# Two graph layers in f32 on one core: the order of the opening steps is changed

## The chip, the cores and the metric

The kernel runs on one core of a Trainium2 chip. The metric is the device time of one execution in microseconds (us); lower is better. The kernel before took a median of 2537.88 us in four runs (2536.48 to 2541.1).

## What is computed

For 64 graphs of 256 nodes with 512 features, two layers follow each other. Each normalises x, applies relu, runs an attention over the same adjacency, and adds the result to x.

```python
h = jnp.maximum(_layernorm(x, axis=-1), 0.0)
x = x + _L0_gnn_ref(h, adj, L0_gnn_W, L0_gnn_a)
h = jnp.maximum(_layernorm(x, axis=-1), 0.0)
x = x + _L1_gnn_ref(h, adj, Wq, bq, Wk, bk, Wv, bv, Wo, bo)
```

Layer 0 forms `h W`, a score for each edge from two columns (`a`), a leaky relu, a masked softmax, and the weighted sum; its output is that sum beside `h W`. Layer 1 is a masked attention with eight heads, with projections q, k, v and an output projection. All arithmetic is in f32.

## The kernel before

**Groups.** The 64 graphs ("batches") are worked in 32 groups of two (`GB`, `NG`). One group passes through these stages:

- `first_norm(g)` (L495 on): statistics of x on VectorE, `rstd` and `less` on GpSimd (`factors`), the normalised `xn` on ScalarE (`norm`), a transposition (`turn`), and the copy `hT0` on ScalarE (`put`). For group 0 the transposition is done by TensorE (tile `pt`). For later groups VectorE turns 32x32 blocks (`xt`, one buffer), a DMA writes them to DRAM (`passed`) and four DMAs bring them back (`moved`, `fetch`).
- `first_layer(g)`: four products `ph` (r0 to r3, two for each batch, with two extra columns for the edge scores), the edge scores `pn` and their exponentials `e`, and four weighted sums `po`, each followed on VectorE by a reciprocal, an add to x and the statistics of the second norm. Then the second norm in the same manner, which ends in `hT1` and in four `operand_sums` on GpSimd (tile `sums`).
- `project(g)`: q, k and v, each from seven products of half size (a Strassen scheme) in the order 1, 2, 6, 7, 5, 4, 3. Products 1, 6, 5 and 3 write one bank (`first`), 7 and 4 another. ScalarE copies a bank out (`take`; the copies that are kept are `kept_q` and so on) before the next product may rewrite it: product 6 waits for the copy of product 1, product 5 for that of 6, product 4 for that of 7. Product 6 is the first one that needs `sums`.
- `scores`, `weigh` and `outputs` (tiles `sc`, `total`, `pr`, `py`): the attention and its output projection.

**Checks on the weights.** `judge()` bounds the sizes of the weights, so that a softmax without a maximum can be used. It forms a gram matrix of the q and of the k weights (`gram_q`, `gram_k`, 32 matmuls each), squares each three times (`square_q`, `square_k`), adds up squares of weights on ScalarE, and ends in a small matmul and a few tiny operations on VectorE and GpSimd. Its verdict is read at the end of the kernel.

**What sets the order.** The order of TensorE's matmuls is the order of the code: each is tied to the one before (`in_order`, helper lines L137 and L140). The functions are generators, and the code at L808 to L890 says by hand which piece comes next. On the other engines most operations are tied behind the last recorded one by `not_sooner`; those that are not tied are placed by the scheduler, and can stand ahead of earlier ones in the code. Each engine works through its finished order one by one. In the opening (groups 0 and 1 in front of the main loop), `order` gives for each product i of `project(0)` what follows it: `n` a piece of `first_norm` (generator `norms`), `s` a piece of `first_layer(1)`; after it comes a piece of `judge()`. At i of 2, 8 and 15 VectorE forms sums of the k, v and o weights (`weight_sums`), and at i of 15 GpSimd adds the last bias to group 0's x (`residual`). In the main loop, `steps` says the same for each quarter of a group: `S` scores, `u` a product of the next group's projections, `o` a piece of the outputs, `s` and `n` as above for the groups two and three further on. All loads are issued on SP's queue, in the order of the code unless a wait lets another go ahead.

Of the kernel before, what the change touches and what calls it, by code (L numbers as in the profile page):

```python
# [10 lines left out]
AF = mybir.ActivationFunctionType  # L11
# [46 lines left out]
def bounded(  # L58
# [24 lines left out]
    vector, scalar, gpsimd, sync = (  # L83
        Remembers(e) for e in (nc.vector, nc.scalar, nc.gpsimd, nc.sync)
    )
# [12 lines left out]
    scale = 1.0 / DH**0.5  # L98
# [10 lines left out]
    def mm(name):  # L109
        return psum.tile([P, 512], F32, tag="turn", name=name, bufs=5)  # L110

    def held_bank(n, name):
        return psum.tile([P, 512], F32, tag=f"held{n}", name=name, bufs=1)

    def after(instruction, name):

        tc.add_manual_dep(
            instruction.ins, name,
            mybir.DependencyInfo(mybir.DependencyClass.NoSync, mybir.DependencyReason.DATA),
            reason="the engine's order",  # L120
        )

    def not_sooner(engine, operation, *args, **kwargs):

        last = engine.last
        after(getattr(engine, operation)(*args, **kwargs), last)
# [9 lines left out]
    def matmul(*args, **kwargs):  # L136
        in_order(nc.tensor.matmul(*args, **kwargs))  # L137
# [9 lines left out]
    def load(g, b):  # L147
        xs[g, b] = big.tile([P, NT, D], F32, tag="x", name=f"x{g}_{b}", bufs=8)
        if g == 2:
            not_sooner(sync, "dma_start", xs[g, b], xg[g, b])  # L150
        else:
            sync.dma_start(xs[g, b], xg[g, b])

    load(0, 0)


    ident = const.tile([P, P], F32, name="ident")
# [7 lines left out]

    w0_sb = const.tile([P, HP, F1 + 2], F32, name="w0_sb")
    nc.sync.dma_start(w0_sb[:, :, 2:], w0.rearrange("(c p) o -> p c o", p=P))
    load(0, 1)
    adj_i = att.tile([P, NT, N], I32, tag="kept", name="adj_i")
    nc.sync.dma_start(adj_i, adj.rearrange("(t p) k -> p t k", p=P))  # L170

# [49 lines left out]
    bcol = {}  # L221
# [30 lines left out]
    def weight_sums(name):  # L252
        w = w_sb[name]
        not_sooner(vector, "tensor_sub", w[:, :, T3, :], w[:, :, W22, :], w[:, :, W12, :])
        vector.tensor_sub(w[:, :, T1, :], w[:, :, W12, :], w[:, :, W11, :])
        vector.tensor_sub(w[:, :, T2, :], w[:, :, W22, :], w[:, :, T1, :])
        vector.tensor_sub(w[:, :, T4, :], w[:, :, W21, :], w[:, :, T2, :])
# [356 lines left out]
    def residual(g):  # L614

        for b in range(GB):
            for t in range(NT):
                xt = xs[g, b][:, t, :]
                not_sooner(gpsimd, "tensor_add", xt, xt, b_out)
# [4 lines left out]
    def place(shape, name):  # L624
        tag = places.pop(0)
        return big.tile(shape, F32, tag=tag, name=name, bufs=1), tag
# [4 lines left out]
    def project(g):  # L631
        ops = operands.pop(g)
        for name in ("q", "k", "v"):
            shape = [P, NT, D] if name == "v" else [P, HP, N]
            dst = {}
            for b in range(GB):
                dst[b], tag = place(shape, f"{name}_{g}_{b}")
                qkv[name, g, b] = dst[b], tag
            turn[0] = 1 - turn[0]

            def blocks(bank):
                return bank.rearrange("p (o n) -> p o n", o=2)

            def product(out, i, start):
                a, w = ops[i][0], w_sb[name][:, :, ops[i][1], :]
                for o in range(2):
                    cols = slice(o * P, (o + 1) * P)
                    for c in range(2):
                        of, by = (a[:, c, cols], w[:, c, :]) if name == "v" else (w[:, c, cols], a[:, c, :])
                        matmul(  # L650
                            out[:, o, :], of, by, start=start and o == c == 0, stop=o == c == 1,
                            skip_group_check=True,
                        )

            def part(b, half):
                if name == "v":
                    return dst[b][:, :, half * D // 2 : (half + 1) * D // 2]
                return dst[b][:, 2 * half : 2 * half + 2, :]

            def take(to, bank, half):  # L660
                if name == "v":
                    scalar.copy(to, bank)
                    return
                for o in range(2):
                    i = 2 * half + o
                    scalar.activation(
                        to[:, o, :], bank[:, o, :], AF.Identity,
                        bias=bcol[name][:, i : i + 1], scale=1.0,
                    )

            def kept(bank, half, i):
                s = att.tile([P, 2, N], F32, tag="kept", name=f"kept{i}_{name}_{g}")
                take(s, bank, half)
                return s

            first = blocks(held_bank(turn[0], f"p{name}1_{g}"))
            product(first, 1, True)
            p1 = kept(first, 0, 0)
            yield
            second = blocks(mm(f"p{name}2_{g}"))  # L680
            product(second, 2, True)
            vector.tensor_add(part(0, 0), second, p1)
            yield
            product(first, 6, False)
            p16 = kept(first, 0, 1)
            yield
            second = blocks(held_bank(1 - turn[0], f"p{name}7_{g}"))
            product(second, 7, True)
            p7 = kept(second, 1, 2)
            yield  # L690
            product(first, 5, False)
            vector.tensor_add(part(1, 1), first, p7)
            yield
            product(second, 4, False)
            vector.tensor_add(part(1, 0), second, p16)
            yield
            product(first, 3, False)
            take(part(0, 1), first, 1)
            yield

# [103 lines left out]
    def run(part):  # L804
        for _ in part:
            pass

    verdict = judge()  # L808
    norms = (piece for g in range(NG) for piece in first_norm(g))
    bias, edges = last_bias(), mask()  # L810
# [6 lines left out]
    for piece, _ in enumerate(first_layer(0)):  # L817
        if piece == 1:
            next(norms)
            next(norms)  # L820
            next(edges)
        elif piece == 2:
            next(norms)
        elif piece == 3:
            next(norms)
            late_loads()
        elif piece in (4, 7, 10):
            next(verdict)
            next(verdict)
            if piece == 10:  # L830
                next(norms)
                next(norms)
                weight_sums("q")
        elif piece == 11:
            next(products)
            next(products)
# [2 lines left out]
    next(norms)  # L839
    next(verdict)  # L840
    next(verdict)
    order = "n - - - nss s s - ss ss s sn n n - sn n n s".split()
    for i, parts in enumerate(order, 2):
        next(products)
        if i in (2, 8, 15):
            weight_sums("kvo"[i // 7])
        for part in parts:
            if part != "-":
                next(norms if part == "n" else pieces, None)
        next(verdict, None)  # L850
        if i in (6, 9, 11):
            next(bias)
        if i == 15:
            residual(0)
# [5 lines left out]
    for g in range(NG):  # L860
        products = project(g + 1) if g + 1 < NG else iter(())
        pieces = first_layer(g + 2) if g + 2 < NG else iter(())
        for step, parts in enumerate(steps):
            b, quad = divmod(step, NQ)
            if waiting is not None:
                weigh(*waiting)
                if waiting[2] == NQ - 1:
                    late = outputs(*waiting[:2])
            for part in parts:
                if part == "u":  # L870
                    next(products, None)
                elif part == "o":
                    next(late, None)
                elif part == "s":
                    next(pieces, None)
                elif part == "n":
                    next(norms, None)
                else:
                    waiting = (g, b, quad, *scores(g, b, quad))
            if step == 0 and g + 1 < NG:  # L880
                residual(g + 1)
            if step % 2 == 0 and g + 3 < NG:
                load(g + 3, b)
        run(products)
        run(pieces)
# [373 lines left out]
```

## Time and profile before

| what | value |
|---|---|
| median of four runs | 2537.88 us |
| the profiled execution's own time | 2537.21 us |
| its span in the profile | 2535.4 us |
| mean granted TensorE clock | 0.998 |
| matmuls | 16158 |
| DMA, mean over the span | 81 GB/s |
| first matmul of group 0's `pt` | 8.42 us |
| first scores `sc` | 97.81 us |
| first `ph` of group 2 | 125.11 us |
| last matmul begins its run at | 2528.74 us |

The profile is that of one execution. PE is TensorE, PEld its weight loads, DVE VectorE, ACT ScalarE, POOL GpSimd, and SP the engine that issues DMAs. A timeline row gives the start, the time until the last of a run of like operations ended, the engine, the line, the operation, the tile that it writes and those that it reads, the shape and the count; in brackets the idle time of the engine before it and what ended it. Nearly all operations show a helper's line (L35, L137, L140), so that the tile's name tells them apart. All times count from the start of the span.

### The profile page before, as it was taken

The numbers are of one execution on the slowest core, as the hardware profiler recorded it, in microseconds if no ns is written. First come the engines' busy times: TensorE is split into PE (matmuls) and PEld (weight loads), VectorE is DVE, ScalarE is ACT, GpSimd is POOL, SyncE is SP. The second block draws the span as 40 slices with busy tenths as digits, with TensorE's granted clock in tenths as the row PEclk, the third lists the DMA queues.
The fourth block names the chain that finished last, engine by engine and source line by source line (L and its number), as shares of the span: only waits on it lengthen the run. The fifth ranks groups of instructions, "written<-read, shape, count | busy, mean of one in ns | idle before, by whom it ended". The sixth has DMA issues, their size and how long they took to land.

```text
span 2535.4 us, 41543 instructions
## 1 busy us (share of the span) xinstructions
PE 2502.8 (99%) x16158; PEld 2027.8 (80%) x16158; DVE 1773.0 (70%) x2971; ACT 1008.9 (40%) x2019; POOL 952.4 (38%) x913
## 2 busy tenths in 40 slices
PE   7999999999999999999999999999999999999998
PEld 6788888888888878887887888788888878888875
DVE  5676766776667777667767677776677676777655
ACT  4443443343343444334443433433444334334321
POOL 3442444333344324443333443243433334433332
PEclk9999999999999999999999999999999999999999
DMA  5221232331222321223312323212233123232100
GB/s 187 67 84 64 69 94 76 100 95 56 75 92 84 100 73 62 92 84 92 100 58 68 100 76 100 80 59 88 84 92 100 59 68 100 75 100 83 38 30 35
DMA packets 129352, 205.39 MB, mean 81 GB/s; under 512 B 13952, under 2 KB 78208, under 8 KB 129152
## 3 DMA queue, kind: packets, MB, share of 16 engines
q1 hardware_dynamic: 129152, 202.69, 25.4%
q8 instruction: 129, 2.11, 0.4%
q14 instruction: 71, 0.58, 0.1%
HBM read 104.08 MB, written 98.57 MB: 80 GB/s over the span
## 4 chain that ended last, share of the span: by engine, by line
PE 97%; DVE 1%; POOL 0%; DMA 0%; ACT 0%; issue 0%; SPq 0%; DVEq 0%; ACTq 0%; POOLq 0%
PE pk L137 16%; PE pv L137 15%; PE pq L137 15%; PE py L137 15%; PE sc L137 10%; PE ph L137 9%; PE pr L137 9%; PE po L137 4%; PE total L137 3%; PE pn L140 1%; DVE p L35 0%; POOL ps L35 0%; ACT xn L35 0%; DVE st L35 0%; DMA moved<-passed 0%
## 5 line engine op out<-in xcount | busy, mean ns | idle before, releaser
L35 POOL TENSOR_TENSOR ps<-p 128x512 f32<-128x512 f32 x256 | 416.6, 1642 | 699.2 <-DVE p L35 699.2
L35 DVE TENSOR_TENSOR x<-py,x 128x256 f32<-128x256 f32 x448 | 186.3, 416 | 314.1 <-PE py L137 307.4
L35 ACT ACTIVATE p<-sc 128x512 f32<-128x512 f32 x512 | 264.3, 603 | 273.7 <-PE sc L137 273.7
L35 DVE TENSOR_TENSOR p<-p,maskT 128x1024 f32<-128x1024 f32 x256 | 335.0, 1339 | 49.6 <-ACT p L35 49.5
L35 ACT ACTIVATE xn<-x,less,rstd 128x512 f32<-128x512 f32 x256 | 194.8, 813 | 308.1 <-POOL less L35 308.1
L137 PE MATMUL sc<-q,k 64*128 64x256 f32 x2048 | 266.8, 391 | 0.0
L137 PE MATMUL py<-wo_sb,o_sums 128*128 128x256 f32 x1024 | 262.8, 380 | 2.6 <-DVE x L35 2.6
L35 DVE RECIPROCAL r<-total 128x256 f32<-128x256 f32 x128 | 224.6, 1755 | 44.6 <-PE total L137 44.6
L137 PEld LDWEIGHTS sc<-q,k 64*128 64x128 f32 x2048 | 196.0, 186 | 72.0 <-issue 52.6
L35 POOL TENSOR_TENSOR rstd<-ve,rexp 128x2 f32<-128x2 f32 x128 | 90.8, 710 | 431.0 <-DVE less L35 430.9
L137 PE MATMUL ph<-w_sb,hT 128*128 128x258 f32 x1024 | 243.5, 386 | 6.0 <-ACT hT L35 3.3
L137 PE MATMUL pr<-p,v 128*32 128x256 f32 x4096 | 245.5, 379 | 0.0
L137 PE MATMUL pq<-sums,wq_sb 128*128 128x256 f32 x1024 | 239.5, 383 | 5.6 <-POOL sums L35 5.6
L137 PE MATMUL pv<-wv_sb,sums 128*128 128x256 f32 x1024 | 241.7, 379 | 0.0
L137 PE MATMUL pk<-sums,wk_sb 128*128 128x256 f32 x1024 | 240.0, 382 | 0.0
L137 PEld LDWEIGHTS ph<-w_sb,hT 128*128 128x128 f32 x1024 | 192.1, 191 | 44.6 <-ACT p L35 9.6
L137 PEld LDWEIGHTS pq<-sums,wq_sb 128*128 128x128 f32 x1024 | 196.7, 192 | 33.0 <-POOL sums L35 6.0
L137 PEld LDWEIGHTS pk<-sums,wk_sb 128*128 128x128 f32 x1024 | 192.0, 190 | 35.6 <-issue 10.7
L137 PEld LDWEIGHTS pv<-wv_sb,sums 128*128 128x128 f32 x1024 | 194.6, 190 | 26.4 <-ACT kept_v L35 0.2
L137 PEld LDWEIGHTS py<-wo_sb,o_sums 128*128 128x128 f32 x1024 | 192.1, 190 | 28.9 <-DVE x L35 3.4
L137 PEld LDWEIGHTS pr<-p,v 128*32 128x32 f32 x4096 | 134.8, 110 | 86.5
L137 PE MATMUL py<-wo_sb,oT 128*128 128x256 f32 x768 | 197.1, 380 | 2.5 <-DVE x L35 2.5
(120 smaller groups left out, 3712.0 us busy)
## 6 DMA issues: line engine op xcount, KB each, us to landing
passed<-xt SPq DMA_DIRECT2D x124, 512.0 KB, 2.7
moved<-passed SPq DMA_DIRECT2D x496, 128.0 KB, 3.5
x<-in_x_dram SPq DMA_DIRECT2D x64, 512.0 KB, 4.8
out_dram<-x SPq DMA_DIRECT2D x64, 512.0 KB, 3.9
wq_sb<-in_L_gnn_Wq_dram SPq DMA_DIRECT2D x2, 512.0 KB, 9.2
wk_sb<-in_L_gnn_Wk_dram SPq DMA_DIRECT2D x2, 512.0 KB, 10.8
wv_sb<-in_L_gnn_Wv_dram SPq DMA_DIRECT2D x2, 512.0 KB, 7.4
wo_sb<-in_L_gnn_Wo_dram SPq DMA_DIRECT2D x8, 128.0 KB, 3.5
```

Of the source, the lines that this page charges most:

```text
L35: instruction = getattr(self.engine, operation)(*args, **kwargs)
L137: in_order(nc.tensor.matmul(*args, **kwargs))
L140: in_order(nc.tensor.transpose(*args))
```

## The change

There are five edits, all in the opening but for one line in the main loop. No matmul, copy or DMA is added or left out.

1. x of group 0's second batch is loaded right behind that of the first, ahead of `a` and `w0`.
2. `gram_k` and the squares move: `gram_q` follows `pn` alone, `gram_k` follows the fourth `po`, and the first pair of squares follows `pt` of the second norm. All later pieces of `judge()` come two steps later.
3. In `order`, pieces of `first_layer(1)` come one or two products later up to its norms, `ph` r2 and r3 behind product 2 of k, `po` behind products 5 and 4 of k. Its last two pieces (the `hT1` copies) stand at i of 17 and 19. The pieces of `first_norm(2)` come later: the first batch's at 15 to 17, the second batch's statistics at 20, and its `xn` and turn behind the first scores in the main loop. `weight_sums("o")` moves from 15 to 19.
4. In the first step of the main loop two `n` stand behind `S`, and the copy of the third group's first batch still follows product 5.
5. In groups 0 and 1 each `take` is tied behind the last recorded operation of ScalarE.

```diff
@@ -152,6 +152,7 @@
     load(0, 0)
+    load(0, 1)
...
@@ -165,7 +166,6 @@
     w0_sb = const.tile([P, HP, F1 + 2], F32, name="w0_sb")
     nc.sync.dma_start(w0_sb[:, :, 2:], w0.rearrange("(c p) o -> p c o", p=P))
-    load(0, 1)
     adj_i = att.tile([P, NT, N], I32, tag="kept", name="adj_i")
...
@@ -658,15 +658,21 @@
             def take(to, bank, half):
+
+                behind = [scalar.last] if g <= 1 else []
                 if name == "v":
-                    scalar.copy(to, bank)
-                    return
-                for o in range(2):
-                    i = 2 * half + o
-                    scalar.activation(
-                        to[:, o, :], bank[:, o, :], AF.Identity,
-                        bias=bcol[name][:, i : i + 1], scale=1.0,
-                    )
+                    taken = [scalar.copy(to, bank)]
+                else:
+                    taken = [
+                        scalar.activation(
+                            to[:, o, :], bank[:, o, :], AF.Identity,
+                            bias=bcol[name][:, 2 * half + o : 2 * half + o + 1], scale=1.0,
+                        )
+                        for o in range(2)
+                    ]
+                for last in behind:
+                    for instruction in taken:
+                        after(instruction, last)
...
@@ -824,13 +830,14 @@
-        elif piece in (4, 7, 10):
+        elif piece == 4 or piece == 9:
+            next(verdict)
+        elif piece == 10:
             next(verdict)
             next(verdict)
-            if piece == 10:
-                next(norms)
-                next(norms)
-                weight_sums("q")
+            next(norms)
+            next(norms)
+            weight_sums("q")
...
@@ -839,10 +846,10 @@
-    order = "n - - - nss s s - ss ss s sn n n - sn n n s".split()
+    order = "n - - - - - nss s s ss ss s s n n sn - s n".split()
     for i, parts in enumerate(order, 2):
         next(products)
-        if i in (2, 8, 15):
+        if i in (2, 8, 19):
             weight_sums("kvo"[i // 7])
...
@@ -862,6 +869,9 @@
             b, quad = divmod(step, NQ)
+            if g == step == 0:
+
+                parts = "Snn" + parts[2:].replace("uon", "unon", 1)
             if waiting is not None:
```

## The prediction

> **What bounds the kernel now.** First the page's busy times, then TensorE's waits, then each engine's timeline for the first 130 us. The page gives TensorE almost the whole span:
>
> ```profile
> PE 2502.8 (99%) x16158; PEld 2027.8 (80%) x16158; DVE 1773.0 (70%) x2971; ACT 1008.9 (40%) x2019; POOL 952.4 (38%) x913
> ```
>
> Of 2535.4 us only 32.6 are idle TensorE. No matmul is removed, so only idle or slowed TensorE can be won. TensorE's waits (total us, times, longest us) say where:
>
> ```profile
> PE pt L140 <- ACT xn L35: 9.5, 2, 8.4
> PE pq L137 <- POOL sums L35: 5.6, 1, 5.6
> PE py L137 <- DVE x L35: 5.0, 4, 1.3
> PE ph L137 <- ACT hT L35: 3.3, 1, 3.3
> PE ph L137 <- issue: 2.7, 1, 2.7
> ```
>
> The py waits lie in the last 50 us, which the edit does not touch. TensorE's own timeline dates the others (start, duration, in brackets the idle time before):
>
> ```profile
> 13.09 5.36 PE L137 MATMUL ph<-w_sb,hT 128*128 128x258 f32 x16 [2.69 <-issue]
> 37.62 1.36 PE L140 MATMUL pt<-ident,xn 128*128 128x128 f32 x8 [1.10 <-ACT xn L35]
> 62.35 3.75 PE L137 MATMUL ph<-w_sb,hT 128*128 128x258 f32 x16 [3.34 <-ACT hT L35]
> 109.03 8.47 PE L137 MATMUL pq<-sums,wq_sb 128*128 128x256 f32 x24 [5.57 <-POOL sums L35]
> ```
>
> So all that can be won lies before 118 us. The last row also hides slow matmuls: 24 of them take 8.47 us, against 5.35 for the same 24 at 50.21, because the granted clock (third figure from the right) fell after the idle stretch:
>
> ```profile
> 108.00:110.00 2.00, 0.97 (x2) 0.59 0.93 257
> 110.00:112.00 2.00, 2.00 (x6) 0.50 0.63 162
> ```
>
> What feeds that wait, from the timelines of ScalarE and GpSimd:
>
> ```profile
> 102.15 1.52 ACT L35 ACTIVATE xn<-x,less,rstd 128x512 f32<-128x512 f32 x2 [2.61 <-POOL less L35]
> 103.58 0.81 ACT L35 ACTIVATE kept_q<-pq,bq_sb 128x256 f32<-128x256 f32 x2
> 104.29 1.13 ACT L35 COPY hT<-moved 128x512 f32<-128x512 f32 x2
> ...
> 105.50 1.27 POOL L35 TENSOR_TENSOR sums<-hT 128x512 f32<-128x512 f32 x1 [3.38 <-ACT hT L35]
> 106.85 2.12 POOL L35 TENSOR_TENSOR sums<-sums,hT 128x512 f32<-128x512 f32 x1
> ```
>
> The second group's hT copy stands behind xn of the third group, whose `less` waited on GpSimd behind residual(0) (96.05 to 101.03). Its transfer had landed about 100.0: the last of four issues began at 96.8, and the median from issue to landing there is 3.3.
>
> [...]5.57 us idle gave 0.50 until about 115, 3.34 us idle (before 62.35) left 1.00. [...]a weight subtraction takes 0.67 alone (wo_sb, 92.32), 1.65 beside GpSimd's sums (wk_sb, 47.70). [...]the trace's landings rose in the order of issue.
>
> **Part 1, x of batch 1 ahead of a and w0.** Before: x(0,0) lands at 4.45, a at 6.75, w0 at 8.85, and batch 1's statistics begin with x(0,1) at 10.21. VectorE then runs 1.88 us of statistics, and only at 12.09 the eight score columns (0.465 each, to 15.79) that gate the 16 ph. After, the same 1.79 MB stand ahead of the end of w0 as stood ahead of x(0,1), so w0 lands about 10.2, the statistics already lie in the idle 6.5 to 10.2, and the columns start 1.9 us sooner. SP issues two DMAs half a microsecond later each, which these bytes contain; adj and all behind see the same bytes ahead. Gain 1.9. Bounds: 0 (w0 lands at 12.1) to 2.3.
>
> **Part 2, gram_k behind po.** Between 23.94 and 44.06 TensorE loses 1.27 us before pt and 0.32 between its halves (two sets of four take 0.88 at 44.06, here 1.20): the norm chain after po r1 has only one pair of squares and two po as cover. After, nothing holds po back when gram_q ends (27.52 in the old time): the first batch's e is masked by 27.1, the second's, needed 1.7 us later, by 27.8; so po follows gram_q, and gram_k (3.58 us) covers VectorE, GpSimd and xn: in shifted time xn's first half ends about 31.9, gram_k at 32.7. The square pairs move back by one place each; their number stays. Gain 1.6; if the cover failed, 0.
>
> **Part 3, order of group 1's pieces.** ph r2, r3 now come two products later (pk1, pk2: 2 x 1.73 = 3.46 us), and one pair of squares (1.78) also moves into that stretch. hT of group 1's second batch comes through xn, weight_sums("k") on VectorE (45.26 to 50.96, stretched by GpSimd), the turn and the round trip, all shifted with TensorE; TensorE arrives 58.9, hT could be there 57.3. But the take of pk1 is now pinned on ScalarE ahead of it, with the squares of wv: 57.25 + 0.82 + 0.63 + 0.2 + 0.58 = 59.5. So 0.6 of the 3.34 us stays: gain 2.7. Bounds 0 and 3.3.
>
> **Part 4, the sums.** po r3 ended at 81.92; after it ends at 81.92 - 1.9 - 1.6 - 2.7 + 1.73 (pk4 now ahead of it) = 77.4. From po r3 to the landing of the second batch took 18.1 us (VectorE, GpSimd, xn, and two round trips that follow each other, as xt has one buffer); none of this is shortened, so landing at 95.5. New is what ScalarE must do then: hT is no longer behind the third group's second xn, but the pins put the take of v, the four exps, that xn and only then kept_q behind hT: 1.14 + 0.58 + 2.06 + 1.52 + 0.82 = 6.1, so product 6, which rewrites kept_q's bank, can start at 101.6. GpSimd is sooner: hT 96.6 + 1.27 + at most 2.12 = 100.0. TensorE, held about 2.2 us at pv6 (kept_v behind xn, one product less as cover), arrives 99 to 100, [...]the clock stays full. Against 109.03: 7.4, of which 6.2 are parts 1 to 3; and the half clock, 8.47 - 5.35 = 3.1.
>
> **Part 5, what is moved past queues.** The third group's second norm issues 1.9 us of VectorE statistics, 0.9 of GpSimd, 1.52 of ScalarE, 1.3 of turning, one 512 KB DMA and, with the fetch, eight of 128 KB on SP. passed went out at 106.35, hT was written by 117.7 at the latest; now about 103.5, so at most 114.9, for ph at 101.6 + 8.65 (five products) + 4.2 (weigh, scores) = 114.5. By the landings (112.9 before, 110 now) 2 to 3 us are left: priced at 0, bounds 0 and 3. weight_sums("o") moves to VectorE ahead of these statistics: 2.7 alone, up to 6.6 beside GpSimd; hidden while `less` is ready by 99. The judge's last pieces come two products later: its `total` then puts GpSimd's 1.96 us power (83.13) at about 3 us behind po r3, ahead of rstd, and may hold the second batch's xn for 0.9; hidden, since the turn behind it waits for the first batch's transfer to land anyway, and the verdict is read only at the end: 0. Pins in group 1's k and v: ScalarE from 124 to 245 already runs in that order (kept_v at 162.14 behind xn at 160.72), with TensorE not idle: 0.
>
> **Sum.** The profiled execution took 2537.21 us (span 2535.4 and 1.8 around it), 0.7 below the median 2537.88. 7.4 + 3.1 = 10.5: 2526.7, on the median's scale **2527.4**.
>
> **Rivals.**
> A: *third group's `less` behind the sums.* If GpSimd's order has all four sums first (6.9 us in this trace, 96.7 to 103.6), then rstd and less 0.9, xn 1.5, kept_q 0.8: product 6 at 107.0, [...]half clock again. Gain 2.0: 2535.9. For it: sums stand first in the code now. Against: rstd has no pin, its statistics should be ready earlier, and GpSimd's operations already leave written order (norm between two rstd at 83.13).
> B: *everything covered.* All idle before 110 and the half clock go: 1.9 + 1.6 + 3.3 + 5.6 + 3.1 = 15.5: 2522.4. Needs the transfers 4 us faster.
> C: *pins stall TensorE.* Each of q, k, v in two groups has three kept copies whose bank is rewritten one or two products (1.73 us each) later: 18 places. If ScalarE's head waits on another engine longer than that cover, TensorE stops behind it. Three stalls are in the sum; at 1.3 us in the other 15 it costs 19.5: 2546. It is slower than before from 0.7 us a place. For: kept_v stood behind xn at 86.94. Against: 124 to 245, above.
> That x earlier does nothing (part 1 at 0) is inside the forecast's own range.
>
> **Chances.** Forecast 0.61 (2524 to 2531), A 0.18, B 0.10, C 0.11. This kernel's measurement can tell about 0.2% (5 us) from no change. Faster: forecast, B and a little of A, 0.73; same: most of A, 0.16; slower: C, 0.11. Range: from B to A, 2522 to 2536.5, leaving out C.
>
> **What would show it.** First ph at 11.2; no idle before pt; ph r2 of group 1 near 59.5 with at most 1 us idle; product 6 of pq near 101.6, waiting for ScalarE rather than GpSimd, and 24 such matmuls in 5.4 us at clock 1.00; ph of the third group near 114.5. Wrong if product 6 starts after 105, if the clock falls to 0.5 there, or if new idle appears between 118 and 245.

## The result and the profile after

The changed kernel takes a median of 2533.48 us (2532.62 to 2534.86), the kernel before 2538.78 (2535.17 to 2541.28): a ratio of 0.998, with a 95% interval of 0.9975 to 0.9985. That is a gain of 5.3 us, in the forecast direction and inside the range, but only half of the 10.5 that were forecast. The profiled execution of the changed kernel took 2535.6 us (span 2533.7), 2.1 above its median, so its trace shows less of the gain than the medians do.

TensorE's waits (total, times, longest, us) in the changed kernel:

```profile
PE pt L140 <- ACT xn L35: 10.3, 1, 10.3
...
PE pq L137 <- POOL sums L35: 4.1, 1, 4.1
PE pv L137 <- ACT kept_v L35: 2.7, 1, 2.7
```

The second wait for xn (1.1), that of the first `ph` (2.7) and most of that of `ph` for hT (3.3, now 0.3) are gone; the first wait for xn is longer (10.3 instead of 8.4). The wait of product 6 of pq for GpSimd's `sums` is still there, 4.1 instead of 5.6, and a wait of 2.7 for `kept_v` is new. TensorE's timeline dates them:

```profile
12.10 5.97 PE L137 MATMUL ph<-w_sb,hT 128*128 128x258 f32 x16
17.91 1.04 PE L140 MATMUL pt<-ident,xn 128*128 128x128 f32 x8
...
61.02 3.75 PE L137 MATMUL ph<-w_sb,hT 128*128 128x258 f32 x16 [0.32 <-ACT hT L35]
...
87.11 7.13 PE L137 MATMUL pv<-wv_sb,sums 128*128 128x256 f32 x24 [2.68 <-ACT kept_v L35]
...
107.35 7.83 PE L137 MATMUL pq<-sums,wq_sb 128*128 128x256 f32 x24 [4.07 <-POOL sums L35]
```

Product 6 of q starts at 107.35, not at the predicted 101.6. Its 24 matmuls take 7.83 us, and those of `pv` at 87.11 (called pv6 from here: the run that begins with product 6 of v) take 7.13, where the same 24 take 5.35 at full clock (as the prediction had it). Two rows of windows (stretch, its length, PE busy with its count of matmuls, granted clock, share of DMA time, GB/s) confirm it for both places:

```profile
88.00:90.00 2.00, 2.00 (x8) 0.58 0.36 112
...
108.00:110.00 2.00, 2.00 (x6) 0.50 0.89 303
```

What feeds the wait at 107.35, first on VectorE, then on GpSimd, then on ScalarE:

```profile
96.61 2.86 DVE L35 TENSOR_TENSOR wo_sb<-wo_sb 128x512 f32<-128x512 f32 x4
99.39 0.69 DVE L35 BATCH_NORM_STATS2 st<-x 128x6 f32<-128x512 f32 x1
...
102.25 0.16 DVE L35 TENSOR_SCALAR less<-mv 128x2 f32<-128x2 f32 x1
```

```profile
102.42 1.68 POOL L35 TENSOR_TENSOR rstd<-ve,rexp 128x2 f32<-128x2 f32 x1 [5.81 <-DVE less L35]
104.18 0.55 POOL L35 TENSOR_TENSOR less<-less,rstd 128x2 f32<-128x2 f32 x1
104.68 1.26 POOL L35 TENSOR_TENSOR sums<-hT 128x512 f32<-128x512 f32 x1
106.03 1.27 POOL L35 TENSOR_TENSOR sums<-sums,hT 128x512 f32<-128x512 f32 x1
```

```profile
98.01 1.14 ACT L35 COPY hT<-moved 128x512 f32<-128x512 f32 x2 [3.26 <-DMA moved<-passed]
...
104.76 1.52 ACT L35 ACTIVATE xn<-x,less,rstd 128x512 f32<-128x512 f32 x2 [3.17 <-POOL less L35]
```

The second batch's hT is copied by 99.2, so GpSimd could form `sums` then. But the third group's `rstd` stands ahead of `sums` in GpSimd's order, it waits 5.81 us for VectorE's statistics, and these stand behind the four subtractions of `weight_sums("o")`. The rows stand in the finished order of three engines; none of the operands of `sums` comes from the third group. ScalarE's `kept_q` is held by the same statistics: it stands behind the third group's xn, which waits for `less`, and its copy lasts from 106.18 to 107.0. So with `sums` out of the way alone, product 6 would still have waited to 107.0.

### The profile page after: what moved, and what is told of

It reads as the page before. It is cut to its first block, busy times and chain, and to the rows that moved or that the text cites. A ratio compares the mean times of both kernels' runs of the same rounds, so it can differ in the third digit from the quotient of the medians.

```text
span 2533.7 us, 41538 instructions
## 1 busy us (share of the span) xinstructions
PE 2504.5 (99%) x16158; PEld 2027.8 (80%) x16158; DVE 1772.0 (70%) x2971; ACT 1009.2 (40%) x2019; POOL 951.7 (38%) x913
## 4 chain that ended last, share of the span: by engine, by line
PE 97%; DVE 1%; POOL 1%; ACT 0%; issue 0%; DMA 0%; DVEq 0%; ACTq 0%; POOLq 0%
PE pq L137 15%; PE pv L137 15%; PE pk L137 15%; PE py L137 15%; PE sc L137 10%; PE ph L137 9%; PE pr L137 9%; PE po L137 4%; PE total L137 3%; PE pn L140 1%; DVE p L35 0%; POOL ps L35 0%; DVE st L35 0%; PE pt L140 0%; ACT xn L35 0%
## 5 line engine op out<-in xcount | busy, mean ns | idle before, releaser
L35 POOL TENSOR_TENSOR rstd<-ve,rexp 128x2 f32<-128x2 f32 x128 | 91.7, 716 | 430.2 <-DVE less L35 430.2
```

What stands on the lines that cost most here:

```text
L35: instruction = getattr(self.engine, operation)(*args, **kwargs)
```

## The experiments

Times are medians, ratios those to runs of the kernel before on the same chip. Before spreads over 8 us (2534.8 to 2542.8), the kernels derived from the changed one over 0.5 to 5 us, so kernels are compared with each other by their medians; ratios can put such a difference 1 to 2 us higher or lower. Where two profiles are compared, times are counted from the second batch's pt (17.91 in the changed kernel), which leaves the start out.

### The place of weight_sums("o")

**wsum_late.** The changed kernel with these four VectorE operations behind the third group's second statistics.

```diff
-        if i in (2, 8, 19):
+        if i in (2, 8):
...
+        if i == 20:
+            weight_sums("o")
```

> Theory: in the changed kernel GpSimd's four sums of group 1 stand behind the third group's rstd, and that waits for statistics which stand on VectorE behind the four o weight sums (96.61 to 99.4). With the weight sums behind the statistics, the rstd's inputs are ready about 2.9 us sooner (99.5 instead of 102.33), the sums start near 100.5 instead of 104.68, product 6 of pq starts near 104.0 instead of 107.35 and is then held by kept_q on ScalarE, the idle stretch is under 1 us and the clock stays full: 3.3 + 2.5 = about 5.8 us less than the changed kernel, 2527.7. Rival (the landing of the second batch sets the sums, the weight sums are hidden): product 6 within 0.5 us of 107.35, no difference in time. Third possibility: start earlier but the clock still halves: 3.3 less.

Measured: 2529.73 us (2529.51 to 2530.04), ratio 0.9961 (0.9947 to 0.9975): 3.75 below the changed kernel. GpSimd and TensorE:

```profile
98.24 1.19 POOL L35 TENSOR_TENSOR rstd<-ve,rexp 128x2 f32<-128x2 f32 x1 [1.98 <-DVE less L35]
...
99.66 1.80 POOL L35 TENSOR_TENSOR sums<-hT 128x512 f32<-128x512 f32 x1
```

```profile
103.83 5.42 PE L137 MATMUL pq<-sums,wq_sb 128*128 128x256 f32 x24 [0.91 <-ACT kept_q L35]
```

`rstd` comes 4.2 us sooner, product 6 waits for ScalarE's `kept_q`, as predicted, and the clock stays full. So the place of four operations of 0.7 us each on VectorE cost 3.8 us on TensorE. That is 2.0 less than the 5.8 expected. The two profiles do show 5.2 at the third group's `ph` (122.78 against 117.18), but in that of the changed kernel the half clock at product 6 lasts 6.8 us; in two others with the same order there, less_first and norm_one_later, it lasts 3.4. A second pair that differs in this move alone, less_first and wsum_late_less_first below, lies 4.1 apart.

**wsum_as_before.** The same operations behind product 15, where the kernel before has them.

```diff
-        if i in (2, 8, 19):
+        if i in (2, 8, 15):
```

> The changed kernel with one move undone: weight_sums of o stands behind product 15 again, as in the kernel before, and so ahead of the third group's first statistics instead of its second ones. If the place to which the change moved these four VectorE operations is what held the third group's less, and through it GpSimd's sums: less near 99.5 instead of 104.7, product 6 near 104 with less than 1.5 us of wait, 24 matmuls in about 5.4 us, and 2529.5 to 2531. They delay the third group's first xn by up to 2.7 us there, which may put the take of v in pv4 later: then up to 2532. Rival, that the order of GpSimd and ScalarE in the change holds the sums in any case: 2533.5, product 6 behind 106.

Measured: 2532.73 us (2531.81 to 2533.74), ratio 0.9977 (0.9968 to 0.9985). That is above what my theory allowed (2532 at most), near the rival's 2533.5. The delay only moves:

```profile
95.20 3.15 PE L137 MATMUL pv<-wv_sb,hT 128*128 128x256 f32 x8 [2.39 <-ACT kept_v L35]
107.48 5.45 PE L137 MATMUL pq<-sums,wq_sb 128*128 128x256 f32 x24 [1.30 <-POOL sums L35]
```

Now the third group's first statistics stand behind `wo_sb`, its first xn comes at 93.2 instead of 91.7 (in an execution that began 1.4 us sooner), and `kept_v`, tied behind that xn, holds product 4 of v for 2.39 us. Ahead of either statistics the four operations are on the path; of the three places tried, only the one behind both takes them off it.

### The place of the judge's last operations

In `wsum_late` another delay showed on VectorE:

```profile
83.11 0.16 DVE L35 TENSOR_TENSOR test<-norm 128x1 f32<-128x1 f32 x1 [1.35 <-POOL norm L35]
...
83.61 1.29 DVE L35 STREAM_TRANSPOSE xt<-xn 128x512 f32<-128x512 f32 x2
```

The first batch's xn was complete at 80.96 (79.44 + 1.52), but its transposes began at 83.61, behind a judge's test that waits for GpSimd's power (tile `norm`, 81.11 to 83.07). The second batch's aggregate stood behind that test too.

**judge_early, judge_earlier.** `wsum_late` with the judge's total two and three products sooner.

```diff
-        for _ in range(3):
+        for _ in range(1):
             yield
         total = mm("total")[:, :10]
```

(In judge_earlier the loop is left out.)

> wsum_late (2529.73) with the judge's total two products earlier, so that GpSimd's power (1.96 us) and VectorE's tests, which wait for it, stand ahead of the second group's last statistics instead of between the first batch's xn and its transposes (79.4 and 83.6 in wsum_late). Theory, that the judge in this place holds both turns: first transposes near 81, second batch's less near 82.5, pv6 with under 1 us of wait and its 24 matmuls in 5.4 us, landing near 95.5, product 6 near 101.5: 2526.5 to 2528. Rival, that the two round trips and po r3 set the landing whatever the judge does, as the prediction had it: landing at 97.5 to 98, 2529 to 2530.

> As judge_early with the total one product earlier still, ahead of po r0. By the same theory at most 0.5 us more, since the chain from po r3 is then free of the judge in both: 2526.5 to 2528. If part's last sum (72 in wsum_late) is not there in time, TensorE waits for it, and the time is up to 1.5 us above judge_early.

Measured: judge_early 2526.49 us (2526.01 to 2527.17), ratio 0.9955 (0.9941 to 0.9968); judge_earlier 2529.16 (2528.27 to 2529.9), ratio 0.9965 (0.9952 to 0.9979). VectorE, ScalarE and TensorE of judge_early:

```profile
81.42 1.30 DVE L35 STREAM_TRANSPOSE xt<-xn 128x512 f32<-128x512 f32 x2
```

```profile
95.95 1.14 ACT L35 COPY hT<-moved 128x512 f32<-128x512 f32 x2 [3.74 <-DMA moved<-passed]
```

```profile
101.80 5.42 PE L137 MATMUL pq<-sums,wq_sb 128*128 128x256 f32 x24 [1.28 <-ACT kept_q L35]
114.83 3.75 PE L137 MATMUL ph<-w_sb,hT 128*128 128x258 f32 x16
```

The transposes begin as soon as xn is complete (79.92 + 1.52). The landing (95.95 against 95.5 predicted), product 6 (101.80 against 101.6) and the third group's `ph` (114.83 against 114.5) are now close to where the prediction had them. In part that is luck: `po` r3 ends at 78.4 instead of 77.4, and the landing behind it (17.6 us, not 18.1) and the copies (5.9, not 6.1) are shorter. Between wsum_late and judge_early lie 3.2 us in the medians (1.5 by the ratios, whose intervals overlap). The profiles show 2.0 of them at the third group's `ph`, once the start (17.55 and 17.20 for the second batch's pt) is taken off. judge_earlier gives 2.7 back, more than the 1.5 allowed for: with the total ahead of `po` r0 TensorE waits 0.54 us for `part`, and VectorE again stands at a test that waits for the power, now ahead of the reciprocals of the first two `po`:

```profile
74.08 0.16 DVE L35 TENSOR_TENSOR test<-norm 128x1 f32<-128x1 f32 x1 [2.10 <-POOL norm L35]
```

The first `rstd` behind `po` comes at 80.72 instead of 78.89. judge_early is the fastest version found, 7.0 us below the changed kernel.

### The start

**less_first, wsum_late_less_first.** At the start of the changed kernel the second batch's `rstd` stands on GpSimd ahead of the first batch's `less`, so that the first pt comes at 10.31 instead of 8.42. Both kernels, the changed one and wsum_late, tie it behind that `less`.

```diff
-            gpsimd.tensor_tensor(rstd, ve, rexp, op=ALU.pow)
+            if name == "0_0" and b == 1:
+                not_sooner(gpsimd, "tensor_tensor", rstd, ve, rexp, op=ALU.pow)
+            else:
+                gpsimd.tensor_tensor(rstd, ve, rexp, op=ALU.pow)
```

> Theory: in the changed kernel the first batch's less stands on GpSimd behind the second batch's rstd (8.51), which delays the first xn from 7.6 to 9.45 and the first transposition from 8.4 to 10.31. Put back ahead of it, the first transposition begins at 8.5 and the first ph near 11.3; but the eight score columns, which now wait for w0 until 10.83, end at 14.5 whatever the transposition does, so ph r1 ends about 16.8 instead of 17.91: 1.1 us less in all. Rival (w0's landing alone sets the start): no difference, below 0.3 us. Rival (the full 1.9 us of the delay comes back): 1.9 us less.

> wsum_late (weight_sums of o behind the third group's statistics, 2529.7) with the first batch's less ahead of the second batch's rstd on GpSimd at the start. Theory, that the order on GpSimd ate part 1: first pt at 8.4 instead of 10.3, second batch's pt near 16.5, 1.0 to 1.5 us sooner than in wsum_late, the rest unchanged: 2528.3 (2527.5 to 2529). Rival, that the score columns' wait for w0 sets the start whatever the norm does: 2529.5 to 2530.

**wsum_late_x_before.** Part 1 undone in wsum_late.

```diff
     load(0, 0)
-    load(0, 1)
...
     nc.sync.dma_start(w0_sb[:, :, 2:], w0.rearrange("(c p) o -> p c o", p=P))
+    load(0, 1)
```

> wsum_late with x of batch 1 loaded behind a and w0 again, as in the kernel before: the worth of part 1 alone. As predicted, part 1 is worth 1.9 us: 2531.6. By the profile of the changed kernel, in which the second batch's pt starts only 0.37 us sooner than before: 2530.1. If the idle stretches around 60 and 86 fall otherwise against the clock's window, up to 2 us either way.

Measured: less_first 2533.71 us (2531.77 to 2536.05), ratio 0.9979 (0.9971 to 0.9986), the changed kernel's own. wsum_late_less_first 2529.64 (2529.11 to 2530.25), ratio 0.9963 (0.9949 to 0.9976), wsum_late's own: the gains of 1.1 and 1.0 to 1.5 did not come. wsum_late_x_before 2530.8 (2530.72 to 2531.96), ratio 0.9969 (0.9957 to 0.9981). Two profiles with the first pt at 8.4 to 8.6, less_first and then wsum_late_less_first:

```profile
10.89 5.75 PE L137 MATMUL ph<-w_sb,hT 128*128 128x258 f32 x16 [0.49 <-issue]
```

```profile
12.29 6.14 PE L137 MATMUL ph<-w_sb,hT 128*128 128x258 f32 x16 [1.68 <-DVE prod L35]
```

The order on GpSimd costs nothing that can be measured: put right, it makes the first `ph` wait instead, in wsum_late_less_first 1.68 us for the score columns (`prod`), as the rival had it.

Part 1 is worth 1.1 us by the medians (2530.8 less 2529.7), 2.0 by the ratios. The profiles scatter: the second batch's pt starts at 16.5 to 17.9, 17.0 in the mean, in the eight whose x comes first and whose order on GpSimd is as changed, and at 18.3 to 19.4, 18.9 in the mean, in the five with x behind w0. Of these 1.9 us, 1.3 are the sooner start of `ph` (12.05 against 13.31 in the mean), and 0.6 its shorter run. Most of the scatter lies in the 16 `ph`, which take 4.6 to 6.7 us; the last section infers why.

### The ties on ScalarE, and where the waits go

**unpinned.** All ties of `take` left out.

```diff
-                behind = [scalar.last] if g <= 1 else []
+                behind = []
```

> Only the ties of the takes behind ScalarE's last operation are gone; the rest of the change stays. Theory: the ties put kept_v of product 1 behind the second batch's xn and so stop TensorE at pv6 for 2.68 us and halve its clock there (7.13 us for 24 matmuls instead of 5.35). Without them kept_v comes ahead, pv6 starts near 84.3, TensorE reaches product 6 of pq near 99, VectorE reaches the third group's statistics 4 us sooner, and the sums are then set by the landing of hT (98.0): product 6 near 102, 5.3 us less than the changed kernel, or 7.8 if the clock stays full there: 2526 to 2528. Rival (GpSimd's sums stay where they are): TensorE only waits longer ahead of product 6, which stays near 107: no difference. Rival (the ties are what gave the gain): slower by 2 us or more.

Measured: 2539.69 us (2538.26 to 2540.44), ratio 1.0001 (0.9993 to 1.0009). The stall at pv6 is gone, but the scheduler then puts other work on GpSimd ahead of `sums`:

```profile
104.84 4.92 POOL L35 TENSOR_TENSOR x<-x,b_out 128x512 f32<-128x512 f32 x4
109.73 1.26 POOL L35 TENSOR_TENSOR sums<-hT 128x512 f32<-128x512 f32 x1
```

Product 6 waits 13.48 us, to 112.38. The time is 12 us above what was expected and 6.2 above the changed kernel, as the third possibility had it. So the ties, which the prediction priced only as stalls and copies on ScalarE, are worth some 6 us here through an order on another engine too: hT's copy came behind xn and `kept_q` without them (103.62), and on GpSimd `sums` came behind `ps` and `residual`. That the scheduler put them there because of the later copy is likely, but not shown.

**norm_one_later.** The second batch's xn one product later, behind `kept_v`.

```diff
-    order = "n - - - - - nss s s ss ss s s n n sn - s n".split()
+    order = "n - - - - - nss s s ss ss - ss n n sn - s n".split()
```

> The ties stay, but the second batch's xn of group 1 comes behind product 1 of v instead of ahead of it, so that kept_v is ahead of xn on ScalarE while xn itself, which waited for less until 85.07, starts no later. Theory: TensorE's wait of 2.68 us at pv6 and the half clock behind it go, TensorE is about 4.4 us sooner at product 6 of pq; VectorE's statistics come sooner, and the sums start at about 99.2; but kept_q stands behind hT, v, four exps and xn, so product 6 starts near 104 after an idle stretch of 5 us with the clock halved: 3.3 us less than the changed kernel, 2530. Rival (sums unmoved): product 6 at 107, no difference. Rival (both free): 7 us less.

**kept_v_free.** wsum_late_less_first with the kept copies of v of the first group untied.

```diff
-            def take(to, bank, half):
+            def take(to, bank, half, free=False):
...
-                behind = [scalar.last] if g <= 1 else []
+                behind = [scalar.last] if g <= 1 and not free else []
...
-                take(s, bank, half)
+                take(s, bank, half, g == 0 and name == "v")
```

> wsum_late_less_first (2529.64) with the three kept copies of v of the first group free of their tie, so that kept_v no longer stands behind xn at 86: the stall of 2.7 us at pv6 and the 1.8 us of half clock behind it go. Theory: product 6 of pq stays set by the landing of the second batch (98) and the copies behind it (103.8), so that TensorE only waits there 4 us longer and loses the clock there instead: 2529 to 2531, with a wait of 4 to 5 us at product 6 and 24 matmuls in over 7 us. Rival, that the stall at pv6 also delays what product 6 waits for: 4 us faster, 2525.5.

Measured: norm_one_later 2533.11 us (2532.12 to 2534.34), ratio 0.9977 (0.9967 to 0.9986); kept_v_free 2531.14 (2529.02 to 2533.96), ratio 0.9971 (0.996 to 0.9982). norm_one_later first, then kept_v_free:

```profile
91.42 2.87 PE L137 MATMUL pv<-wv_sb,hT 128*128 128x256 f32 x8 [3.20 <-ACT kept_v L35]
```

```profile
104.50 7.98 PE L137 MATMUL pq<-sums,wq_sb 128*128 128x256 f32 x24 [5.47 <-ACT kept_q L35]
```

Without the stall at pv6 TensorE waits elsewhere. In norm_one_later it waits at product 4 of v, and product 6 of q still waits for `sums` behind `weight_sums("o")` (105.67); its time is the changed kernel's but for 0.4 us, as the rival with unmoved sums had it. In kept_v_free it waits at product 6 of q, whose time is set by the landing and the copies behind it, and loses the clock there (7.98 us for 24 matmuls): 1.5 us more than wsum_late_less_first. So the new 2.7 us of wait and the 1.8 of half clock behind it cost nothing while product 6 is as late as it is.

### The second and third part, and the kernel before

**wsum_late_grams_before.** Part 2 undone in wsum_late, with the judge's steps where they were.

```diff
-        elif piece == 4 or piece == 9:
-            next(verdict)
-        elif piece == 10:
+        elif piece in (4, 7, 10):
             next(verdict)
             next(verdict)
-            next(norms)
-            next(norms)
-            weight_sums("q")
+            if piece == 10:
+                next(norms)
+                next(norms)
+                weight_sums("q")
```

> wsum_late (2529.73) with gram_k ahead of the first po again and the squares in their old places: part 2 undone, all else kept. As predicted part 2 is worth 1.6: 2531.3, the second pt at 35.5 to 36 instead of 33.83 with 1.1 us of wait for xn, and everything behind it as much later. Rival, that po r3 and the chain of copies behind it set product 6 whatever stands ahead: product 6 still at 103.8 and 2529.7.

Measured: 2530.96 us (2529.3 to 2532.54), ratio 0.9971 (0.9959 to 0.9983), 1.2 above wsum_late. Product 6 is at 103.89, as the rival said, but with a start 0.95 sooner than in wsum_late's profile. The 1.2 is not the worth of the gram matrices: with its steps where they were, the judge's total stands at 77.44, behind the second `po`, where judge_early has it (74.71), and that by itself gains. Against judge_early this kernel is 4.5 us slower (4.1 by the ratios), and 3.3 in the profiles at the third group's `ph` (117.50 less 16.60 against 114.83 less 17.20). Of these, 1.3 come from the second norm's pt and 2.0 from `ph` of the second group, which waits 2.28 us instead of 0.32: on ScalarE hT's copy (62.41) stands behind nine squares of weights of the judge, which in the change come two steps later, behind that copy (65.08 against 60.35).

**ph_later_only.** The kernel before with the pieces of `first_layer(1)` up to `po` as in part 3, and nothing else of the change.

```diff
-    order = "n - - - nss s s - ss ss s sn n n - sn n n s".split()
+    order = "n - - - - - nss s s ss ss s sn n n sn n n s".split()
```

> The kernel before with part 3 alone: ph r2 and r3 of the second group two products later. TensorE's wait of 3.3 us at 62 becomes 0.3 to 0.6; po r3 ends only some 1.3 us sooner, since one more product stands ahead of it, so product 6 starts 1.3 us sooner with a longer wait ahead of it. By lengths alone 2539 less 1.3: 2537.7. If the wait of 3.3 us lowers the clock in most executions of before (as in before_again_2, 2540.4, and not in before_again_1, 2535.7), those lose another 3 us: 2534 to 2535, without the executions near 2540.

Measured: 2537.56 us (2535.27 to 2539.11), ratio 0.9993 (0.9986 to 0.9999). The time is near the 2537.7 that lengths alone gave, but the wait is not: 2.09 us of it stay where 0.3 to 0.6 were expected, since hT's copy (64.91) stands behind the same squares of the judge (60.78 to 64.9).

**before_again_1, before_again_2.** The kernel before, unchanged.

> The kernel before, unchanged, profiled a second time. Its profiled execution showed a stretch of 3.34 us without matmuls ahead of 62.35 that left the clock at 1.00, while 2.68 us in the changed kernel were enough for 0.5. If the clock is lowered by the place of the idle stretch[...], this execution may show 0.5 for about 3.5 us behind 62; then the third group's first ph is about 3 us later (128 instead of 125.1) and the time 2539 to 2541. If it is lowered by the length alone, the clock stays at 1.00 there and the time is 2535.5 to 2537.5.

> As before_again_1, a third look at the same kernel: [...]the executions at 2537 to 2541 are those with 0.5 behind 62, and those at 2535 to 2537 have 1.00 there. With the length alone, the spread of before has another cause, and the clock behind 62 is the same in all.

Measured: 2535.66 and 2540.44 us. before_again_1, before_again_2 and ph_later_only at the `ph` of the second group:

```profile
62.40 3.75 PE L137 MATMUL ph<-w_sb,hT 128*128 128x258 f32 x16 [2.92 <-ACT hT L35]
```

```profile
63.49 6.69 PE L137 MATMUL ph<-w_sb,hT 128*128 128x258 f32 x16 [3.32 <-ACT hT L35]
```

```profile
65.56 5.44 PE L137 MATMUL ph<-w_sb,hT 128*128 128x258 f32 x16 [2.09 <-ACT hT L35]
```

In the prediction's profile a wait of 3.34 us left the clock full; in before_again_2 one of 3.32 halved it, 3 us are lost there, and the whole execution is 4.8 longer than before_again_1. In ph_later_only 2.09 us are enough for the half clock. So the length of a wait alone does not decide; in these traces it goes by where the wait falls on a grid of 3.41 us in the clock's record (the last section has the figures). In these two executions the half clock makes 3 of 4.8 us. How much of the spread of before it explains is not shown: the prediction's own profile, with the clock full there, took 2537.2, and ph_later_only still ranges over 3.8 us.

## Why the prediction was right in part, and where it failed

The step that failed is part 5: two moved pieces were priced at zero, and cost 3.8 us and 2.0 to 3.2.

**Part 1** was priced at 1.9. The means over the profiles give 1.9, the times 1.1 to 2.0, and the one profile of the changed kernel only 0.4 (17.91 against 18.28), since its 16 `ph` took 5.97 us. The mean agrees partly by luck: `ph`, predicted at 11.2, came at 12.1, in the mean 1.3 us sooner than with x behind w0; the other 0.6 are shorter matmuls, by the clock as the last section infers it, which the prediction did not have.

**Part 2**, 1.6, held in size for what it named: in the profiles, with the moved pair of squares (1.78) taken off, the second norm's pt comes 1.3 us nearer to the start (wsum_late against wsum_late_grams_before). It left out what the judge's later steps do elsewhere: they keep its squares off hT's copy, 2.0 us won at `ph`, and hold the transposes, 2.0 to 3.2 lost (part 5).

**Part 3** held for the wait it names: 0.32 us of 3.34 stay, `ph` at 61.02 instead of 59.5, and the 1.5 between are the start's. It holds only together with the judge's later steps; without them 2.09 us stay (ph_later_only, which gives 1.1 us) or 2.28 (wsum_late_grams_before).

**Part 4** was right about its chain and wrong about the clock. Behind the landing the copies take 5.9 us (wsum_late: 97.97 to 103.83; predicted 6.1), and product 6 waits for `kept_q`. The stall at pv6 was predicted at 2.2 and came at 2.7. "the clock stays full" failed at pv6, because a wait's length was taken as the measure (3.34 us had left 1.00): 2.68 us were enough, and left TensorE idle for 0.65 of one window on the grid of the clock's record (last section). kept_v_free shows that this cost nothing.

**Part 5** has the two prices of zero.

- "weight_sums("o") ... hidden while `less` is ready by 99". `less` was ready at 104.7. The prediction has no layout of VectorE's queue for these operations: they could start only at 96.61, behind the last add of v, and the statistics behind them at 99.39. Moved behind the statistics, they free 3.8 us by the medians (wsum_late); in the profiles 3.2 of wait and 2.4 of half clock, of which the changed kernel's profiled execution had more than others.
- The judge's total "may hold the second batch's xn for 0.9; hidden, since the turn behind it waits for the first batch's transfer". What was missed is VectorE: the test that reads the power stands ahead of the first batch's own transposes, so that the first transfer, the cover, was late as well. Out of the way, it gives 3.2 us by the medians, 2.0 in the profiles (judge_early).

Together the two make up 7.0 us between the changed kernel and judge_early (6.3 by the ratios).

The sum closes at product 6 of the profile: 101.6 predicted, 1.5 from that execution's start, 1.0 from the judge (the landing 19.1 behind `po` r3, not 18.1), 0.2 less for the copies, and from `weight_sums("o")` what is left of 107.35, some 3.4; wsum_late shows 3.2 of it as wait. The 2.4 of half clock behind it were in the sum as won. With both orders mended the kernel takes 2526.49. By its ratio, 0.9955, that is a gain of 11.4 where 10.5 was forecast.

**The rivals.** A (third group's `less` sets product 6, at 107.0 with the half clock) came nearest in time, but with the opposite order: not `sums` ahead of `rstd`, as A had it, but `rstd` ahead of `sums`. B and C did not occur; C's stalls showed once, at pv6. (A's terms add up to 106.8, not 107.0, and C's 2546 is on the profile's scale; on the median's it is 2546.9. Neither matters here.) The third group's own norm and the ties between 118 and 245 cost nothing, as priced: the trace of the changed kernel lists no wait of TensorE there.

## What to carry to other kernels

When an operation is moved "behind" others on an engine that works through its rows in order (`sums`, whose hT was copied by 99.2, ran at 104.68, behind `rstd`), lay the whole queue of that engine out with times up to the next thing that someone waits for: four short weight operations cost 3.8 us here, and a test of 0.16 us 2.0 to 3.2, because a norm's statistics and transposes stood behind them. A cover must be followed to its own source: the transfer that was to hide the judge was itself held by the judge. Before a wait is taken away, ask what sets the next one; here stalls at pv6, at `ph` and at product 4 could be exchanged for a longer wait at product 6 with changes of 0.4 to 1.5 us in time. And a kernel that undoes one part of a change has to undo that part alone: wsum_late_grams_before moved the judge as well, and its 1.2 us were the difference of two larger effects.

## What was not expected of the hardware

- The same wait can cost 3 us of half clock or nothing: 3.34 and 2.92 us left 1.00 at 62, 3.32 halved it; 2.09 halved it at 65.56, and 2.28 at 63.06 in wsum_late_grams_before left 16 matmuls at 3.75 us. The clock's record in the traces shows where they differ. Until the last matmul its stretches at 0.50 last 3.41, 6.83 or 13.65 us (the last in unpinned, where the clock is 0.66 in the mean from 100 to 120), and they begin on a grid of 3.41 us that runs on from its first entry and lies elsewhere in each execution: from 16.63 us in the changed kernel, where they begin 21 and 26 steps later (88.31 and 105.37), from 16.20 in the profile before, where one begins 27 steps later (108.36). In all 16 profiles, each window of that grid at full clock in which TensorE was idle (by its matmul rows, whose ends are modelled) for 0.59 of the time or more (0.59 in before_again_1, at the start of its wait of 5.57) was followed by half clock, and none with 0.52 or less (0.52 in the profile before, from 60.57). The 3.34 us fell on two windows (0.46 and 0.52 idle), the 3.32 mostly on one (0.73 and 0.24), the 2.09 on one (0.61), the 2.28 on two (0.30 and 0.36). The clock came back after a window that was idle for at most 0.16 (0.16 in ph_later_only, behind its wait of 5.36), and stayed at half after 0.20 or more (0.20 in the profile before, from 108.36). As an estimate from these figures, a wait of 2.0 us (0.59 of 3.41) can be enough where it falls into one window, and one of 3.5 (twice 0.52) can pass where it falls on two evenly.
- The first 16 `ph` take 4.6 to 6.7 us, against 3.72 for the next 16, though the windows print a granted clock of 1.00 there. The record has no entry that early: its first one, at full clock, comes between 13.4 and 18.3 us, at 16.6 in the changed kernel. With TensorE at half rate up to that entry the 16 `ph` of the changed kernel would take 3.72 + (16.63 - 12.10) / 2 = 5.99 us, and took 5.97. The same sum is right within 0.1 us in 15 of the 16 profiles; judge_earlier, whose entry comes first, took 0.4 more; there the score columns, which end at 14.3, may hold the first eight. That the clock was at half there is inferred from this agreement, not recorded.
